# Moving attention coefficients by one pixel: three shift matmuls replaced by two SBUF-to-SBUF transfers per block

## The chip, the core and the metric

The kernel runs on one core of a Trainium2 chip. A core has five engines with instruction queues of their own: TensorE (PE, matmuls, with weight loads shown apart as PEld), VectorE (DVE), ScalarE (ACT), GpSimd (POOL) and SyncE (SP), which here only issues transfers. They run side by side and wait for each other by semaphores. Transfers are carried out by 16 DMA engines. The metric is the device time of one execution in microseconds (us), lower is better.

## What is computed

The reference is a network of two layers on an image batch of 4 x 32 x 32 pixels with 384 channels; each layer is a token mixer ("conv") and a feed-forward part. Only the second layer's mixer, an outlook attention with 12 heads, is touched:

```python
v = jnp.einsum('bhwc,oc->bhwo', x, Wv)
vp = jnp.pad(v, ((0, 0), (1, 1), (1, 1), (0, 0)))
patches = jnp.stack([vp[:, i:i + h, j:j + w] for i in range(3) for j in range(3)], axis=3)
a = jnp.einsum('bhwc,oc->bhwo', x, Wa).reshape(b, n, heads, 9, 9)
attn = jax.nn.softmax(a * d ** (-0.5), axis=-1)
out = jnp.einsum('bnhpq,bnqhd->bnphd', attn, v_unf)
# each of the 9 results p = (i, j) is added to the canvas at offset (i, j), the borders are cut off
y = canvas[:, 1:1 + h, 1:1 + w]
return jnp.einsum('bhwc,oc->bhwo', y, Wo)
```

Each pixel has, per head, 9 x 9 softmax coefficients. What a pixel's output takes from a pixel up to two rows and two columns away is a sum of such coefficients over the centre pixels between them. So the result is a banded product: a band of 25 coefficients per pixel and head times v.

## The kernel before

Before this stage, the first layer's attention (to about 1220 us) and its experts (to about 2358 us) run; after it, the second feed-forward part, which is factored (from about 2825 us). The stage in between is the function `outlook`, from 2360 to 2826 us. It works on blocks of 128 pixels (4 image rows of 32), 8 blocks an image (`NB`), 32 blocks in all; a pixel is a partition. Its parts, each a local function:

- `scores(b, t)`: normalizes the block (`xn`), transposes it on PE (`xnT`), multiplies it with `wa` into PSUM (`ps_a`, L1728), subtracts the maximum (L1737, L1738), takes the exponential on ACT (L1743), sums (L1745 to L1749), takes the inverse (L1750), and multiplies (L1752) into the tile `attn`. It then sends the coefficients of the upper and lower centre rows to the pixels of the image row above or below, that is by 32 partitions: L1764 and L1765 inside the block (96 partitions each), L1767 and L1769 into the neighbouring blocks (32 partitions each). Their targets are the tiles `up` and `down`. It also computes v (L1772, L1776).
- `band(b, t)`: adds what came from above, from below and its own part into `u` (L1785 to L1789), `u` being split by the three horizontal positions of a coefficient. Then three matmuls (L1793) with 128 x 128 shift matrices move the three parts by -1, 0 and +1 pixel, that is by one partition, and add them in PSUM (`ps_c`); the shift matrices have zero rows at the image's edges. DVE copies the result to `co` (L1801) and masks with `inside` what would fall outside of the image. `co` is written to a DRAM area (`room`, L1808), 150 KB, with a row pitch that puts each coefficient where the band wants it; L1814 reads the band back, 1,560 KB, with rows that overlap as memory is read.
- `gather(b, half, t)`: the banded product of v with the band on PE (`ps_y`, L1830). When half an image is complete, ACT copies it to `y` (L1839).
- `mix`: multiplies with `wo` (`ps_wo`, L1846) and adds to x (L1850).
- `add`: for the last blocks, adds the experts' results (gathered by POOL, L1483) to x (L1701).

Steps: a table `later` says which part runs in which step. In step s, `scores` of block s come first, then loads and `add`, then what the table has: `band` of block s - 2, `gather` of block s - 5 (`LAG` = 3), and `mix` after half an image is complete. The order of the instructions on SP and POOL is this program order (`manual_schedule`); on PE, DVE and ACT a planner chooses the order beforehand, and the engine keeps it. [...] SP issues in each step four moves (L1764 to L1769), the room write, which waits for `co`, and the band read, which waits until the room write has landed.

Buffers: `attn` 3, `up` and `down` 4 each, `u` 2, `co` 3, `band` 5, v 7; in PSUM one of `ps_a` (two banks), one of `ps_c`, three of `ps_y`, two shared by `ps_tr`, `ps_v` and `ps_wo`.

Of the kernel before, what the change touches and what calls it, by code (L numbers as in the profile page):

```python
# [1629 lines left out]
def outlook(net, wv, wa, wo, left, router, kron, loads):  # L1630
# [10 lines left out]
    tc, nc = net.tc, net.nc  # L1641
    K2, H6 = 9, NH // 2
    HW_ = K2 * K2 * H6
    PW = K2 * H6
    R = 5 * NH
    with ExitStack() as ctx:
        const = ctx.enter_context(tc.tile_pool(name="ol_const", bufs=1, reuse_waits="tile"))
        work = ctx.enter_context(tc.tile_pool(name="ol_work", bufs=2, reuse_waits="tile"))
        mp = ctx.enter_context(tc.tile_pool(name="ol_moved", bufs=4, reuse_waits="tile"))
        ap_ = ctx.enter_context(tc.tile_pool(name="ol_attn", bufs=3, reuse_waits="tile"))  # L1650
        vp = ctx.enter_context(tc.tile_pool(name="ol_v", bufs=7, reuse_waits="tile"))
        bp = ctx.enter_context(tc.tile_pool(name="ol_band", bufs=5, reuse_waits="tile"))
        ps_m = ctx.enter_context(tc.tile_pool(name="ol_ps_m", bufs=2, space=PSUM, reuse_waits="tile"))
        ps_a = ctx.enter_context(tc.tile_pool(name="ol_ps_a", bufs=1, space=PSUM, reuse_waits="tile"))
        ps_c = ctx.enter_context(tc.tile_pool(name="ol_ps_c", bufs=1, space=PSUM, reuse_waits="tile"))
        ps_y = ctx.enter_context(tc.tile_pool(name="ol_ps_y", bufs=1, space=PSUM, reuse_waits="tile"))


        shift = {}
        for dx in (-1, 0, 1):  # L1660
            m = const.tile([P, P], FP, name=f"shift_{dx}", tag=f"shift_{dx}")
            nc.gpsimd.memset(m, 0.0)
            nc.gpsimd.affine_select(
                out=m, in_=m, compare_op=ALU.not_equal, fill=1.0,
                base=dx, pattern=[[-1, P]], channel_multiplier=1,
            )
            if dx:
                edge = 0 if dx == 1 else IMG - 1
                nc.gpsimd.memset(m.rearrange("p (r x) -> p r x", x=IMG)[:, :, edge : edge + 1], 0.0)
            shift[dx] = m  # L1670

        inside = const.tile([P, 5 * H6], FP, name="inside")
        col = const.tile([P, 4], FP, name="col")
        low = const.tile([P, 5 * H6], FP, name="low")
# [1 line left out]
        def columns():  # L1676
            nc.gpsimd.iota(
                col[:, 0:1], pattern=[[0, 1]], base=0, channel_multiplier=1, allow_small_or_imprecise_dtypes=True,
            )
            for r in range(1, P // IMG):  # L1680
                nc.vector.tensor_scalar(
                    col[:, r : r + 1], col[:, 0:1], IMG * r - 0.5, -float(IMG), ALU.is_gt, ALU.mult
                )
            for r in range(1, P // IMG):
                nc.vector.tensor_tensor(col[:, 0:1], col[:, 0:1], col[:, r : r + 1], ALU.add)
            nc.gpsimd.iota(
                inside, pattern=[[1, 5], [0, H6]], base=-2, channel_multiplier=0,
                allow_small_or_imprecise_dtypes=True,
            )
            nc.vector.tensor_scalar(inside, inside, col[:, 0:1], None, ALU.add)  # L1690
            nc.vector.tensor_scalar(low, inside, -0.5, None, ALU.is_gt)
            nc.vector.tensor_scalar(inside, inside, IMG - 0.5, None, ALU.is_lt)
            nc.vector.tensor_tensor(inside, inside, low, ALU.mult)

        left = list(left)

# [6 lines left out]
                )  # L1703
            net.measure(work, i, net.x(i))

        attn, vs, bands, ys, moved = {}, {}, {}, {}, {}

        def room(b, t):

# [8 lines left out]
        def scores(b, t):  # L1718
# [11 lines left out]
                        start=k == 0, stop=k == KC - 1,  # L1730
                    )

            a = ap_.tile([P, 3, 2, 3, PW], FP, name="attn", tag="attn")
            for hh in range(2):
                mx = work.tile([P, PW], FP, name="a_max", tag="a_max")
                given = pa[:, hh, :HW_].rearrange("p (q e) -> p q e", q=K2)
                nc.vector.tensor_reduce(mx, given.rearrange("p q e -> p e q"), AX.X, ALU.max)  # L1737
                nc.vector.tensor_tensor(  # L1738
                    a[:, :, hh, :, :], given.rearrange("p (y x) e -> p y x e", y=3),
                    mx.unsqueeze(1).unsqueeze(1).to_broadcast([P, 3, 3, PW]), ALU.subtract,  # L1740
                )
            flat = a.rearrange("p y s x e -> p (y s x e)")
            nc.scalar.activation(flat, flat, AF.Exp, scale=QK_SCALE)  # L1743
            rows = work.tile([P, 2, 3, PW], FP, name="a_rows", tag="a_rows", bufs=1)
            nc.vector.tensor_tensor(rows, a[:, 0], a[:, 1], ALU.add)  # L1745
            nc.vector.tensor_tensor(rows, rows, a[:, 2], ALU.add)
            sm = work.tile([P, 2, PW], FP, name="a_sum", tag="a_sum")
            nc.vector.tensor_tensor(sm, rows[:, :, 0, :], rows[:, :, 1, :], ALU.add)
            nc.vector.tensor_tensor(sm, sm, rows[:, :, 2, :], ALU.add)  # L1749
            nc.vector.reciprocal(sm, sm)  # L1750
            for qi in (0, 2, 1):
                nc.vector.tensor_tensor(  # L1752
                    a[:, qi], a[:, qi], sm.unsqueeze(2).to_broadcast([P, 2, 3, PW]), ALU.mult
                )
            attn[b, t] = a


            flat = [a[:, qi].rearrange("p s x e -> p (s x e)") for qi in range(3)]
            if t == 0:
                moved[b, 0] = room(b, 0)  # L1760
            if t + 1 < NB:
# [13 lines left out]
            v = vs[b, t] = vp.tile([P, C], FP, name="v", tag="v")  # L1775
            nc.scalar.copy(v, ps[:, :C])  # L1776

        def band(b, t):


            H3 = 3 * H6
            u = work.tile([P, 6, 5, H3], FP, name="u", tag="u")
            down, up = (m.rearrange("p (g y e) -> p g y e", g=6, y=3) for m in moved.pop((b, t)))
            own = attn.pop((b, t))[:, 1].rearrange("p s x (y e) -> p (s x) y e", y=3)
            nc.scalar.copy(u[:, :, 0, :], down[:, :, 0, :])  # L1785
            nc.scalar.copy(u[:, :, 4, :], up[:, :, 2, :])
            nc.vector.tensor_tensor(u[:, :, 1:3, :], down[:, :, 1:3, :], own[:, :, 0:2, :], ALU.add)
            nc.vector.tensor_tensor(u[:, :, 3, :], own[:, :, 2, :], up[:, :, 1, :], ALU.add)
            nc.vector.tensor_tensor(u[:, :, 2, :], u[:, :, 2, :], up[:, :, 0, :], ALU.add)  # L1789
            pc = ps_c.tile([P, 512], FP, name="ps_c", tag="c")  # L1790
            grid = pc[:, : 5 * R].rearrange("p (s y e) -> p s y e", s=2, y=5)
            for qj in (1, 0, 2):
                nc.tensor.matmul(  # L1793
                    grid[:, :, :, (2 - qj) * H6 : (5 - qj) * H6],
                    lhsT=shift[qj - 1],
                    rhs=u.rearrange("p (s x) y e -> p s x y e", s=2)[:, :, qj, :, :],
                    start=qj == 1, stop=qj == 2, skip_group_check=True,
                )
            co = work.tile([P, 5, 5, NH], FP, name="co", tag="co", bufs=3)
            for hh in range(2):  # L1800
                nc.vector.tensor_tensor(  # L1801
                    co[:, :, :, hh * H6 : (hh + 1) * H6],
                    grid[:, hh].rearrange("p y (x h) -> p y x h", x=5),
                    inside.rearrange("p (x h) -> p x h", x=5).unsqueeze(1).to_broadcast([P, 5, 5, H6]),
                    ALU.mult,
                )
            room = net.room[t]
            nc.sync.dma_start(  # L1808
                out=room.rearrange("(p r) -> p r", p=P)[:, : 5 * IMG * NH]
                .rearrange("p (y r) -> p y r", y=5)[:, :, :R],  # L1810
                in_=co.rearrange("p y x h -> p y (x h)"),
            )
            m = bands[b, t] = bp.tile([P, BAND, NH], FP, name="band", tag="band")
            nc.sync.dma_start(  # L1814
                out=m.rearrange("p t h -> p (t h)"),
                in_=room[: P * BAND * NH].rearrange("(p r) -> p r", p=P),
            )
# [37 lines left out]
        def at(step, f, *args):  # L1855
            later.setdefault(step, []).append((f, args))
# [12 lines left out]
        for b in range(B):  # L1869
            for t in range(NB):  # L1870
                o = b * NB + t
                at(o + 2, band, b, t)
                at(o + 2 + LAG, gathered, b, 0 if t < 5 else 1, t)
                if t == 4:
                    at(o + 2 + LAG, gathered, b, 1, 3)
                    at(o + 2 + LAG, gathered, b, 1, 4)
            for half in range(2):
                done = b * NB + (4 if half == 0 else 7) + 2 + LAG
                for n in range(4):
                    at(done + 1 + n // 2, mixed, b, half, n)  # L1880
        assert left[0] >= 2 * NB
        t_kron, first = 0, left[0]
        for step in range(B * NB + 9):
            b, t = divmod(step, NB)
            if b < B:
                scores(b, t)
            if step == 0:
                columns()
            if step in loads:
                loads[step]()  # L1890
            if step >= 4 and left:
# [340 lines left out]
```

## Time and profile before

| | |
|---|---|
| median of 3 runs | 2922.51 us (2905.18 to 2929.6) |
| profiled execution, its own time | 2919.42 us |
| its span | 2917.6 us |
| PE busy in the span | 2761.2 us (95%) |
| DVE, ACT, POOL busy | 46%, 41%, 14% |
| the stage `outlook` | 2360 to 2826 us, PE busy 441.6 us |
| L1793, the shift matmuls: PE busy in the stage | 35.7 us |
| SP's transfers in the stage, a block | 4 moves, 1 room write, 1 band read |

In a row of a group, the first name is the line, then the engine, the operation, output and inputs, shapes, and the count; behind the bar stand the busy time and the mean of one instruction in ns, behind the next one the idle time of the engine just before them, with what ended it. A row of the timeline has the start, the duration, engine, line, operation, operands and count; what stands in brackets is the idle time before it and what ended it. A row of waits reads: who waited, for whom, us in all, how often, the longest. For SP ("SPq") a duration is that of the issue, not of the transfer.

### The profile page before, as it was taken

How to read it: one execution, taken by the hardware profiler on the slowest of the kernel's cores; microseconds unless marked ns; L12 is line 12 of the kernel's file. 1: busy time of each engine (PE TensorE's matmuls, PEld its weight loads, DVE VectorE, ACT ScalarE, POOL GpSimd, SP SyncE). 2: the span in 40 equal slices, each digit the busy share in tenths (PEclk: the TensorE clock that was granted, in tenths of full speed). 3: DMA queues.
4: the chain of work that ended last, by engine and by line, in shares of the span. 5: the costliest groups of instructions: out<-in, count | busy, mean ns of one | idle time of the engine just before them, and what ended most of it. 6: DMA issues, size and time to landing. Idle time of an engine off the chain costs nothing. (4 is left out here: it accounts for less than half of the span.)

```text
span 2917.6 us, 36735 instructions
## 1 busy us (share of the span) xinstructions
PE 2761.2 (95%) x13236; PEld 1505.9 (52%) x13236; DVE 1347.7 (46%) x3714; ACT 1207.3 (41%) x2023; POOL 400.6 (14%) x499
## 2 busy tenths in 40 slices
PE   6989999999999998699999999999999998999988
PEld 4333333333334332267777777777777754444432
DVE  1376667777777776533000001111111146877642
ACT  3788677677768775211111211211211122122125
POOL 1000000110030004123111122122221101100000
PEclk9999999999999988699999999999999999999999
DMA  5143335223322234345454455555655437544432
GB/s 103 39 115 91 89 90 139 66 62 78 100 55 62 78 79 124 112 163 217 161 195 179 174 203 191 213 201 204 222 190 214 154 130 224 192 154 158 151 105 89
DMA packets 216992, 405.92 MB, mean 139 GB/s; under 512 B 83504, under 2 KB 177904, under 8 KB 203744
## 3 DMA queue, kind: packets, MB, share of 16 engines
q1 hardware_dynamic: 185504, 189.20, 21.6%
q0 software_dynamic: 27152, 209.66, 20.8%
q10 hardware_dynamic: 4144, 4.61, 0.5%
q8 instruction: 107, 1.75, 0.2%
q14 instruction: 85, 0.70, 0.1%
HBM read 305.35 MB, written 49.99 MB: 122 GB/s over the span
## 5 line engine op out<-in xcount | busy, mean ns | idle before, releaser
L1604 ACT ACTIVATE h<-ps_h,up 128x256 f32<-128x256 f32 x420 | 198.6, 473 | 915.2 <-PE ps_h L1600 915.1
L1600 PE MATMUL ps_h<-xbT,up 128*128 128x256 f32 x2520 | 553.2, 380 | 2.6 <-ACT h L1604 1.8
L1617 PE MATMUL ps_y<-down,h 128*128 128x384 f32 x1680 | 554.9, 488 | 0.0
L1600 PEld LDWEIGHTS ps_h<-xbT,up 128*128 128x128 f32 x2520 | 480.7, 191 | 76.7 <-ACT h L1604 2.7
L678 DVE CUSTOM_DVE_ANT_0 e<-e,rz,inv 128x1024 f32<-128x1024 f32 x384 | 475.2, 1274 | 30.0 <-DMA rz<-r_row 30.0
L626 ACT ACTIVATE e<-ps_s,shift 128x1024 f32<-128x1024 f32 x384 | 408.6, 1109 | 81.2 <-PE ps_s L616 48.7
L1617 PEld LDWEIGHTS ps_y<-down,h 128*128 128x128 f32 x1680 | 318.0, 191 | 206.6 <-issue 1.8
L1622 DVE TENSOR_TENSOR y<-ps_y,down 128x384 f32<-128x384 f32 x70 | 39.0, 558 | 721.1 <-PE ps_y L1617 721.1
L616 PE MATMUL ps_s<-q,k 32*128 32x512 f32 x1536 | 279.0, 664 | 36.4 <-ACT e L626 26.7
L634 PE MATMUL ps_o<-e,wv 128*32 128x512 f32 x1536 | 228.4, 670 | 39.3 <-DVE wv L685 36.7
L634 PE MATMUL ps_z<-e,rt_ones 128*32 128x512 f32 x1536 | 218.6, 643 | 0.0
L705 POOL DMA_DIRECT2D q<-po x96 | 76.1, 875 | 958.4 <-DMA q<-po 600.5
L366 ACT ACTIVATE below<-tk_left,tk_bound 128x1024 bf16<-128x1024 f32 (+1 forms) x160 | 184.3, 1152 | 38.0 <-DVE tk_bound L372 31.7
L1728 PE MATMUL ps_a<-wa,xnT 128*128 128x486 f32 x384 | 170.6, 594 | 8.9 <-DVE attn L1738 7.1
L616 PEld LDWEIGHTS ps_s<-q,k 32*128 32x128 f32 x1536 | 84.1, 189 | 168.7 <-ACT e L626 82.6
L281 PE MATMUL ps_t<-xnT,wqkv 128*128 128x512 f32 x288 | 135.4, 611 | 1.1 <-ACT q L520 0.7
L634 PEld LDWEIGHTS ps_o<-e,wv 128*32 128x32 f32 x1536 | 31.7, 112 | 200.3 <-issue 72.6
L1728 PEld LDWEIGHTS ps_a<-wa,xnT 128*128 128x128 f32 x384 | 73.1, 196 | 95.6 <-issue 87.1
L634 PEld LDWEIGHTS ps_z<-e,rt_ones 128*32 128x32 f32 x1536 | 52.7, 118 | 131.1 <-issue 127.1
L1830 PE MATMUL ps_y<-band,v 128*32 128x194 f32 (+2 forms) x960 | 102.7, 516 | 7.2 <-DMA band<-room 6.9
L1569 DVE SCALAR_TENSOR_TENSOR x<-yt,weight,x 128x384 f32<-128x384 f32 x38 | 23.5, 619 | 185.4 <-DMA x<-x 184.7
L1483 POOL DMA_INDIRECT yt<-yg,index x64 | 65.7, 1027 | 304.6 <-DVE x L1569 139.9
(345 smaller groups left out, 2859.2 us busy)
## 6 DMA issues: line engine op xcount, KB each, us to landing
band<-room SPq DMA_DIRECT2D x32, 1560.0 KB
rz<-r_row SPq DMA_DIRECT2D x48, 512.0 KB
yg<-y SPq DMA_DIRECT2D x70, 192.0 KB
q<-q SPq DMA_DIRECT2D x192, 64.0 KB
k<-k SPq DMA_DIRECT2D x192, 64.0 KB
room<-none SPq DMA_DIRECT2D x64, 192.0 KB
x<-x SPq DMA_DIRECT2D x38, 192.0 KB
o<-in_x_dram SPq DMA_DIRECT2D x33, 192.0 KB
```

Source lines behind the costliest of these rows:

```text
L281: nc.tensor.matmul(ps, lhsT=lhsT(k), rhs=rhs(k), start=k == 0, stop=k == KC - 1)
L366: nc.scalar.activation(junk[:n], left[:n], AF.Sign, bias=bound[:n], accum_out=over[:n])
L616: nc.tensor.matmul(ps[:, half * 512 : half * 512 + 512], lhsT=self.k4[r, u * P : (u + 1) * P], rhs=self.q4[r, :], start=True, stop=True,)
L626: nc.scalar.activation(e, ps, AF.Exp, bias=shift, scale=QK_SCALE)
L634: nc.tensor.matmul(ps[r : r + 32, :], lhsT=lhsT(odd), rhs=self.es[2 * u + odd][:, half * 512 : half * 512 + 512], start=u == 0, stop=u == ...
L678: nc.vector.tensor_tensor_reduce(self.es[m], self.es[m], self.rz, 1.0, self.im["inv"][:, m, self.h : self.h + 1], ALU.mult, ALU.add, self. ...
L705: nc.gpsimd.dma_start(out=there, in_=po[r : r + 32, :], accum_op=ALU.add)
L1600: nc.tensor.matmul(ps, lhsT=up[:, o : o + P], rhs=xbT[:, k, :], start=k == 0, stop=k == KC - 1,)
L1604: nc.scalar.activation(h, ps, AF.Gelu, bias=up[:, KC * HID + f : KC * HID + f + 1])
L1617: nc.tensor.matmul(ps, lhsT=hs[f][:, t * P : (t + 1) * P], rhs=down[:, f * C : (f + 1) * C], start=f == 0, stop=f == NF - 1,)
L1728: nc.tensor.matmul(pa[:, hh, :HW_], lhsT=xnT[:, k, :], rhs=wa[:, k, hh * HW_ : (hh + 1) * HW_], start=k == 0, stop=k == KC - 1,)
L1830: nc.tensor.matmul(ys[c][32 * n : 32 * n + 32, lo - 512 * half : hi - 512 * half], lhsT=vs[b, t][:, h * HD : (h + 1) * HD], rhs=bands[b, t ...
```

## The change

The function `band` is cut in two. The new first half, `column(b, t)`, runs in step s for block s - 2; it makes `u` as before and then sends two parts of it to neighbouring pixels: the parts of horizontal position 0 from partitions 1 to 127 to partitions 0 to 126, and those of position 2 from partitions 0 to 126 to partitions 1 to 127. Each is a transfer on SP of 127 partitions with 180 values (720 bytes) in a partition. The targets are two tiles `beside`, used in turn and zeroed once. The new `band` runs one step later, for block s - 3: it builds `co` in SBUF from its own part and the two that have come, with two copies on ACT and four sums on DVE. In a step's order `band` of block s - 3 stands ahead of `column` of block s - 2. `gather` and `mix` run one step later too, so the loop has one step more, and v has 8 buffers in place of 7.

The masks at the image's edges now are multiplied into the inverse of the softmax sums (`edge`, a constant tile made in `columns`), so that coefficients that would leave the image are zero from the start. For that, the inverse is spread over the three horizontal positions (one more product of 324 elements on DVE), and the tile `attn` has its axes in the order position, head group. The three shift matrices, the PSUM tile `ps_c` and the masked copies go. `columns` is called ahead of the first `scores`.

```diff
-        vp = ctx.enter_context(tc.tile_pool(name="ol_v", bufs=7, reuse_waits="tile"))
+        vp = ctx.enter_context(tc.tile_pool(name="ol_v", bufs=8, reuse_waits="tile"))
...
-        shift = {}
-        for dx in (-1, 0, 1):
...
+        H3 = 3 * H6
+        beside = [const.tile([P, 2, 2, 5, H3], FP, name=f"beside_{n}", tag=f"beside_{n}") for n in range(2)]
+        for m in beside:
             nc.gpsimd.memset(m, 0.0)
...
+        edge = const.tile([P, 3, 2 * 3, H3], FP, name="edge")
...
+            targets = inside[:, H6 : 4 * H6].unsqueeze(1).to_broadcast([P, 2 * 3, H3])
+            for qj in range(3):
+                source = inside[:, (qj + 1) * H6 : (qj + 1) * H6 + 1]
+                nc.vector.tensor_scalar(edge[:, qj], targets, source, None, ALU.mult)
...
             nc.vector.reciprocal(sm, sm)
+            nc.vector.tensor_tensor(
+                rows, edge.rearrange("p x (s y) e -> p x s (y e)", s=2),
+                sm.unsqueeze(1).to_broadcast([P, 3, 2, PW]), ALU.mult,
+            )
             for qi in (0, 2, 1):
-                nc.vector.tensor_tensor(
-                    a[:, qi], a[:, qi], sm.unsqueeze(2).to_broadcast([P, 2, 3, PW]), ALU.mult
-                )
+                nc.vector.tensor_tensor(a[:, qi], a[:, qi], rows, ALU.mult)
...
-        def band(b, t):
+        def column(b, t):
...
-            pc = ps_c.tile([P, 512], FP, name="ps_c", tag="c")
-            grid = pc[:, : 5 * R].rearrange("p (s y e) -> p s y e", s=2, y=5)
-            for qj in (1, 0, 2):
-                nc.tensor.matmul(
-                    grid[:, :, :, (2 - qj) * H6 : (5 - qj) * H6],
-                    lhsT=shift[qj - 1],
-                    rhs=u.rearrange("p (s x) y e -> p s x y e", s=2)[:, :, qj, :, :],
-                    start=qj == 1, stop=qj == 2, skip_group_check=True,
-                )
+            m = beside[t % 2].rearrange("p k s y e -> p k (s y e)")
+            nc.sync.dma_start(out=m[: P - 1, 0, :], in_=u[1:, 0:2].rearrange("p s y e -> p (s y e)"))
+            nc.sync.dma_start(out=m[1:, 1, :], in_=u[: P - 1, 4:6].rearrange("p s y e -> p (s y e)"))
+
+        def band(b, t):
+
+            u, m = us.pop((b, t)), beside[t % 2]
             co = work.tile([P, 5, 5, NH], FP, name="co", tag="co", bufs=3)
-            for hh in range(2):
-                nc.vector.tensor_tensor(
-                    co[:, :, :, hh * H6 : (hh + 1) * H6],
-                    grid[:, hh].rearrange("p y (x h) -> p y x h", x=5),
-                    inside.rearrange("p (x h) -> p x h", x=5).unsqueeze(1).to_broadcast([P, 5, 5, H6]),
-                    ALU.mult,
-                )
+
+            def part(source, pj):
+                return source[:, :, :, pj * H6 : (pj + 1) * H6]
+
+            before, own, behind = m[:, 1], u[:, 2:4], m[:, 0]
+            there = [co[:, :, x, :].rearrange("p y (s h) -> p s y h", s=2) for x in range(5)]
+            nc.scalar.copy(there[0], part(before, 0))
+            nc.scalar.copy(there[4], part(behind, 2))
+            for x in (1, 2):
+                nc.vector.tensor_tensor(there[x], part(own, x - 1), part(before, x), ALU.add)
+            nc.vector.tensor_tensor(there[3], part(own, 2), part(behind, 1), ALU.add)
+            nc.vector.tensor_tensor(there[2], there[2], part(behind, 0), ALU.add)
             room = net.room[t]
...
-                at(o + 2, band, b, t)
-                at(o + 2 + LAG, gathered, b, 0 if t < 5 else 1, t)
+                at(o + 3, band, b, t)
+                at(o + 2, column, b, t)
+                at(o + 3 + LAG, gathered, b, 0 if t < 5 else 1, t)
...
-        for step in range(B * NB + 9):
+        columns()
+        for step in range(B * NB + 10):
```

More of the change, by code (lines that the diff above doesn't have):

```diff
@@ L1654, in outlook @@
         ps_a = ctx.enter_context(tc.tile_pool(name="ol_ps_a", bufs=1, space=PSUM, reuse_waits="tile"))
-        ps_c = ctx.enter_context(tc.tile_pool(name="ol_ps_c", bufs=1, space=PSUM, reuse_waits="tile"))
         ps_y = ctx.enter_context(tc.tile_pool(name="ol_ps_y", bufs=1, space=PSUM, reuse_waits="tile"))
-        shift = {}
-        for dx in (-1, 0, 1):
-            m = const.tile([P, P], FP, name=f"shift_{dx}", tag=f"shift_{dx}")
+        H3 = 3 * H6
+        beside = [const.tile([P, 2, 2, 5, H3], FP, name=f"beside_{n}", tag=f"beside_{n}") for n in range(2)]
+        for m in beside:
             nc.gpsimd.memset(m, 0.0)
-            nc.gpsimd.affine_select(
-                out=m, in_=m, compare_op=ALU.not_equal, fill=1.0,
-                base=dx, pattern=[[-1, P]], channel_multiplier=1,
-            )
[L1667 to L1670, printed above, removed]
+        edge = const.tile([P, 3, 2 * 3, H3], FP, name="edge")
         inside = const.tile([P, 5 * H6], FP, name="inside")
@@ L1704, in add @@
             net.measure(work, i, net.x(i))
-        attn, vs, bands, ys, moved = {}, {}, {}, {}, {}
+        attn, us, vs, bands, ys, moved = {}, {}, {}, {}, {}, {}
         def room(b, t):
@@ L1731, in scores @@
                     )
-            a = ap_.tile([P, 3, 2, 3, PW], FP, name="attn", tag="attn")
+            a = ap_.tile([P, 3, 3, 2, PW], FP, name="attn", tag="attn")
             for hh in range(2):
@@ L1738, in scores @@
                 nc.vector.tensor_tensor(
-                    a[:, :, hh, :, :], given.rearrange("p (y x) e -> p y x e", y=3),
+                    a[:, :, :, hh, :], given.rearrange("p (y x) e -> p y x e", y=3),
                     mx.unsqueeze(1).unsqueeze(1).to_broadcast([P, 3, 3, PW]), ALU.subtract,
                 )
-            flat = a.rearrange("p y s x e -> p (y s x e)")
+            flat = a.rearrange("p y x s e -> p (y x s e)")
             nc.scalar.activation(flat, flat, AF.Exp, scale=QK_SCALE)
-            rows = work.tile([P, 2, 3, PW], FP, name="a_rows", tag="a_rows", bufs=1)
+            rows = work.tile([P, 3, 2, PW], FP, name="a_rows", tag="a_rows", bufs=1)
             nc.vector.tensor_tensor(rows, a[:, 0], a[:, 1], ALU.add)
@@ L1747, in scores @@
             sm = work.tile([P, 2, PW], FP, name="a_sum", tag="a_sum")
-            nc.vector.tensor_tensor(sm, rows[:, :, 0, :], rows[:, :, 1, :], ALU.add)
-            nc.vector.tensor_tensor(sm, sm, rows[:, :, 2, :], ALU.add)
+            nc.vector.tensor_tensor(sm, rows[:, 0], rows[:, 1], ALU.add)
+            nc.vector.tensor_tensor(sm, sm, rows[:, 2], ALU.add)
             nc.vector.reciprocal(sm, sm)
+            nc.vector.tensor_tensor(
+                rows, edge.rearrange("p x (s y) e -> p x s (y e)", s=2),
+                sm.unsqueeze(1).to_broadcast([P, 3, 2, PW]), ALU.mult,
+            )
             for qi in (0, 2, 1):
-                nc.vector.tensor_tensor(
-                    a[:, qi], a[:, qi], sm.unsqueeze(2).to_broadcast([P, 2, 3, PW]), ALU.mult
-                )
+                nc.vector.tensor_tensor(a[:, qi], a[:, qi], rows, ALU.mult)
             attn[b, t] = a
-            flat = [a[:, qi].rearrange("p s x e -> p (s x e)") for qi in range(3)]
+            flat = [a[:, qi].rearrange("p x s e -> p (x s e)") for qi in range(3)]
             if t == 0:
@@ L1776, in scores @@
             nc.scalar.copy(v, ps[:, :C])
-        def band(b, t):
-            H3 = 3 * H6
-            u = work.tile([P, 6, 5, H3], FP, name="u", tag="u")
+        def column(b, t):
+            u = us[b, t] = work.tile([P, 6, 5, H3], FP, name="u", tag="u")
             down, up = (m.rearrange("p (g y e) -> p g y e", g=6, y=3) for m in moved.pop((b, t)))
-            own = attn.pop((b, t))[:, 1].rearrange("p s x (y e) -> p (s x) y e", y=3)
+            own = attn.pop((b, t))[:, 1].rearrange("p x s (y e) -> p (x s) y e", y=3)
             nc.scalar.copy(u[:, :, 0, :], down[:, :, 0, :])
@@ L1789, in band @@
             nc.vector.tensor_tensor(u[:, :, 2, :], u[:, :, 2, :], up[:, :, 0, :], ALU.add)
-            pc = ps_c.tile([P, 512], FP, name="ps_c", tag="c")
-            grid = pc[:, : 5 * R].rearrange("p (s y e) -> p s y e", s=2, y=5)
-            for qj in (1, 0, 2):
-                nc.tensor.matmul(
-                    grid[:, :, :, (2 - qj) * H6 : (5 - qj) * H6],
-                    lhsT=shift[qj - 1],
-                    rhs=u.rearrange("p (s x) y e -> p s x y e", s=2)[:, :, qj, :, :],
-                    start=qj == 1, stop=qj == 2, skip_group_check=True,
-                )
-            co = work.tile([P, 5, 5, NH], FP, name="co", tag="co", bufs=3)
-            for hh in range(2):
-                nc.vector.tensor_tensor(
-                    co[:, :, :, hh * H6 : (hh + 1) * H6],
-                    grid[:, hh].rearrange("p y (x h) -> p y x h", x=5),
-                    inside.rearrange("p (x h) -> p x h", x=5).unsqueeze(1).to_broadcast([P, 5, 5, H6]),
-                    ALU.mult,
-                )
+            m = beside[t % 2].rearrange("p k s y e -> p k (s y e)")
[3 more added lines that the diff above has]
+            u, m = us.pop((b, t)), beside[t % 2]
+            co = work.tile([P, 5, 5, NH], FP, name="co", tag="co", bufs=3)
+            def part(source, pj):
[8 more added lines that the diff above has]
+            nc.vector.tensor_tensor(there[2], there[2], part(behind, 0), ALU.add)
             room = net.room[t]
@@ L1871, in outlook @@
                 o = b * NB + t
-                at(o + 2, band, b, t)
-                at(o + 2 + LAG, gathered, b, 0 if t < 5 else 1, t)
+                at(o + 3, band, b, t)
+                at(o + 2, column, b, t)
+                at(o + 3 + LAG, gathered, b, 0 if t < 5 else 1, t)
                 if t == 4:
-                    at(o + 2 + LAG, gathered, b, 1, 3)
-                    at(o + 2 + LAG, gathered, b, 1, 4)
+                    at(o + 3 + LAG, gathered, b, 1, 3)
+                    at(o + 3 + LAG, gathered, b, 1, 4)
             for half in range(2):
-                done = b * NB + (4 if half == 0 else 7) + 2 + LAG
+                done = b * NB + (4 if half == 0 else 7) + 3 + LAG
                 for n in range(4):
@@ L1886, in outlook @@
                 scores(b, t)
-            if step == 0:
-                columns()
             if step in loads:
```

## The prediction

> **What bounds the kernel now.** I read the page first, then the busy time by stretch of the last conv stage (2360 to 2826 us, the only stage that the diff touches), then the chain of waits inside it, the waits of SP's queue, and SP's timeline. The stretches:
>
> ```profile
> 2360.00:2560.00 200.00, 183.51 (x758) 91.53 (x757) 145.82 (x355) 41.46 (x84) 25.37 (x28) 0.96 0.60 187
> 2560.00:2782.00 222.00, 222.00 (x1018) 108.06 (x1019) 156.62 (x395) 51.56 (x100) 1.08 (x3) 1.00 0.47 155
> 2782.00:2826.00 44.00, 36.09 (x248) 18.66 (x241) 21.34 (x56) 6.37 (x11) 0.00 (x0) 0.92 0.41 140
> ```
>
> Columns: stretch, length, then busy us of PE, weight loads, VectorE (DVE), ScalarE (ACT), GpSimd (POOL), granted clock, DMA share, GB/s. PE has no gap at all for 222 us; DVE is busy 71% of it. The stage is PE-bound in its middle, with 16.5 us of PE idle in its head and 8 us in its tail. The groups by form give what the change removes, and the prices I shall use:
>
> ```profile
> L1793 PE MATMUL ps_c<-u,shift 128*128 128x180 f32 x128 | 31.1, 324 | 0.9 <-DVE u L1789 0.9
> L1752 DVE TENSOR_TENSOR attn<-attn,a_sum 128x324 f32<-128x324 f32 x96 | 41.8, 489 | 0.6
> L1801 DVE TENSOR_TENSOR co<-ps_c,inside 128x150 f32<-128x150 f32 x64 | 17.9, 307 | 29.1 <-PE ps_c L1793 29.1
> L1789 DVE TENSOR_TENSOR u<-u,up 128x108 f32<-128x108 f32 x32 | 8.3, 263 | 0.0
> ```
>
> Now the queue that the change adds to. SP issues in program order; one step of its timeline in the steady part, and the drain at the end:
>
> ```profile
> 2647.64 0.54 SPq L1764 DMA_DIRECT2D up<-attn  x1
> 2648.28 0.55 SPq L1765 DMA_DIRECT2D down<-attn  x1
> 2648.88 0.59 SPq L1767 DMA_DIRECT2D up<-attn  x1
> 2649.52 0.58 SPq L1769 DMA_DIRECT2D down<-attn  x1
> 2650.15 0.58 SPq L1808 DMA_DIRECT2D room<-co  x1
> 2652.74 0.33 SPq L1814 DMA_DIRECT2D band<-room  x1
> 2662.90 0.54 SPq L1764 DMA_DIRECT2D up<-attn  x1
> ...
> 2800.34 0.32 SPq L1814 DMA_DIRECT2D band<-room  x1
> 2800.76 0.39 SPq L1808 DMA_DIRECT2D room<-co  x1
> 2807.64 0.32 SPq L1814 DMA_DIRECT2D band<-room  x1
> ```
>
> In the steady step the coefficients' write to DRAM (room) has landed 2.6 us after its issue, and the band's read goes out. In the drain the same room transfer needs 6.9 us, because it stands behind the 1.56 MB band issued 0.4 us earlier. So whatever SP issues right after a band waits for that band. SP itself has room today:
>
> ```profile
> SPq L1764 <- DVE attn L1752: 202.1, 32, 16.1
> SPq L1814 <- DMA room<-co: 91.8, 32, 6.9
> ```
>
> 202.1/32 = 6.3 us a step in which SP only waits for the next coefficients.
>
> [...] Each engine used leaves one 4-byte packet: SP's queue has 1,146 transfers and 17,760 such packets, 576 short of 16 each, which is 48 x 12: the 48 transfers at L650, whose slowest dimension is 4. No transfer of 127 partitions is in it. [...]
>
> **The change, part by part.**
>
> *Removed, PE.* Three shift matmuls a block; from the first to the next instruction's start is 1.02 us in the timeline (2644.73 to 2645.75), 32 x 1.02 = 33 us of the PE-bound stage. That is the gain if nothing else bounds.
>
> *DVE.* The two masked copies go (2 x 0.28 = 0.56 us); the masked inverse comes (324 elements, 0.49), and four sums of 60 elements, [...] 0.88. Net +0.8 us a block, 26 us in all, under DVE's 29% idle while PE bounds; 26 us is its price if that cover is gone, and nothing less than 0 is possible, since no row shortens. The new order of axes leaves every element count as it was. ACT gets two copies of 60 elements, under 0.28 each (108 elements take that), with ACT busy 23%.
>
> *Set-up.* The shift matrices' memsets and selects leave POOL (1.6 us at 2311), two memsets of 360 elements come (an estimate of 0.45 each, from 0.20 for 128 elements), the iotas move ahead of one memset of 0.36; `edge` costs DVE 3 x 0.27. All lie under the experts' last tile, where PE has 48 matmuls from 2342.5 to 2358; without that cover, 2 us. The eighth v buffer pays for the later gather and costs nothing.
>
> *Two transfers a block on SP, and a step more.* Issue: 2 x 0.55 = 1.1 us a step of SP's 6.3 idle. They wait for u of their block, which is long done; behind them on SP stand the next block's four moves, then the room write, which waits for co, which waits for these two transfers. Their data is the dispute. They are [127 partitions x 720 B], [...] 254 packets on the same engine. The packet records give the price of one: 18 ns for 240 B, 56 ns for 1,296 B, 65 for 1,536; the line through the first two gives 35 ns for 720 B, 254 x 35 = 9.0 us. Bounds: the band's 12,480 B take 467 ns, at that rate 720 B would take 27 ns (6.9 us); no more than a 1,296 B packet, 56 ns (14.2 us). I take 9.0.
>
> *The loop that this makes.* SP's order in a step becomes: four moves, room, band, then the two column transfers. A move's landing sets the fixed part: issued at 2648.28, its reader is released at 2650.64, 2.4 us, of which 0.55 is issue and 6 x 56 ns packets; of the other 1.5 I put 1.0 behind the packets. Let a band be issued at 0. Its reader starts 6.6 us later in the drain (2800.34 to 2806.93), so engine 0 is through with it at about 5.6. The column packets end at 14.6 and land at 15.6. co: 4 x 0.22 and a hand-over, 1.0, gives 16.6. Room to band, 2.6: the next band at 19.2. That is the bare cycle; with the packet bounds 17.1 to 24.4. Today a step is 13.3 us ((2787.91 - 2375.97)/31). A longer cycle is possible: co waits on DVE, in order, and the softmax of the next block may stand behind it there (two sums of rows 0.98, two of 0.27, inverse 0.82, masked inverse 0.49, first product 0.49: 3.3 us), and its moves, 2.45 us, stand ahead of the room write on SP. With all of that in the way it is 5.8 us more, with nothing in the way 0; I take half, 3.0: 22.2 us.
>
> *The sum.* The first band goes out at 2402.75 today; its two transfers now come first, behind the x loads, 12 us by the same reckoning: 2415. Then 28 cycles of 22.2 = 622, the last 3, with no softmax left, of 19.2 = 58, and 8 us for the x and weight loads (2.3 MB at the band's rate) that pass between: last band at 3103, against 2807.64 today. From there to the end nothing changes. +295 us on the profiled execution's 2919.4 (span 2917.6; 3 us below the runs' median of 2922.5, which I neglect): **3215 us**. PE's 33 us are not in the sum: PE then waits, with (441.6 - 33)/32 = 12.8 us of work in a step of 22.2.
>
> **The rivals.**
>
> 1. *The transfers spread over 16 engines, or cost little.* Each then has 8 packets an engine, 0.3 us. The cycle would be 5.6 + 0.6 + 1.0 + 1.0 + 2.6 = 10.8, under PE's 12.8, and the PE gain shows: -33, less a longer drain. From the last moves to the last band take 19.7 us today (2787.91 to 2807.64); then it is 4.8 to the first band and three cycles, 37.2: +17.5, of which 5 us are filled by the gather and mix that come a step later; and six steps without gather instead of five, in which DVE has 9.0 us against PE's 7.7, cost 8. -33 + 17.5 - 5 + 8 = -12.5: about 2907. This is the case on the other side (not slower). It decides from the point where both transfers together take under 12.8 - 10.2 = 2.6 us, i.e. from 4 engines on. For it: every other transfer of this stage uses 16. [...]
> 2. *Spread, but DVE's order holds up co.* Rival 1's cycle and the full 5.8 us: 16.6 against 13.3 now, in the blocks where it happens. If a third of them do, 10 x 3.3 = 33 less the 12.5: about 2940.
> 3. *One engine and dearer packets, or further waits of DVE and SP in turn.* 56 ns and 5.8 us: 28 x 30.2 + 3 x 24.4 + 2423 = 3342, 534 later: 3453, and beyond. For it: a quarter of the 1,296 B packets took 81 ns or more. Against: those were among bursts on all engines.
>
> **How the numbers follow.** The forecast with its bounds (packets of 27 to 56 ns, DVE's part 0 to 5.8 us) has 0.82; rival 1 0.07; rival 2 0.05; rival 3 beyond its bound 0.06. The low end is 31 x 17.1 + 2423 = 2953, +145: 3060; the high end, a little inside rival 3's sum, 3430. That holds 8 in 10, all on one side. About 1% is what a measurement of this kernel tells from no change: faster by more than that (below 2893) 0.03, the better part of rival 1; within it 0.09, the rest of rival 1 and rival 2; slower 0.88.
>
> **What would show it.** Right: SP's wait for co turns from 35 us into the largest one, 8 us a step or more; co and the two copies wait for the moved columns by DMA; bands are issued some 22 us apart; PE is busy little over half of the stage; 4-byte packets fall short of 16 a transfer by 64 x 15 more. Each step can fail alone: landing of the columns 9 us behind the band's end (packets), DVE's share (cycle against 19.2). Wrong: the columns land within 8 us of the band's issue, steps stay near 13 us, and PE stays at 100%[...].

## The result and the profile after

The changed kernel takes 3129.21 us (median of 4 runs, 3123.32 to 3139.93) against 2923.01 us (4 runs, 2905.18 to 2929.6) beside it on the same chip: a ratio of 1.073 [1.0701, 1.0759], slower by 206 us. The prediction was 3215 us with a range of 3060 to 3430 and a chance of 0.88 for slower. The profiled execution took 3128.58 us, its span 3126.8 us. The stage begins 4.5 us later than before (first move at 2380.51 us, not 2375.97); the last band goes out at 3019.58 us instead of 2807.64, and 107.2 us later the span ends (110.0 before). So nearly all of the difference lies in the stage that the diff touches, between its first move and its last band.

Two stretches of it, in the columns of the prediction's first view (length, busy us of PE, weight loads, DVE, ACT, POOL, then clock, DMA share, GB/s):

```profile
2460.00:2660.00 200.00, 139.93 (x547) 62.39 (x545) 113.66 (x295) 35.29 (x78) 19.60 (x22) 0.85 0.43 140
2660.00:2860.00 200.00, 146.05 (x608) 67.00 (x609) 109.44 (x293) 37.82 (x85) 0.72 (x2) 0.85 0.37 122
```

PE, 100% busy in the middle of the stage before, is now busy 70 to 73%, and that at a granted clock of 0.85 instead of 1.00. No compute engine is near its limit. DMA, with a share of 0.4, isn't either, but that is an average over 16 DMA engines, and an average can't show one of them being full. What the end waits for is shown by the chain (the page's fourth part, by line):

```profile
DMA beside<-u 6%; SPq L1787 2%; DMA room<-co 2%; SPq L1761 2%; DMA up<-attn 1%; PE ps_h L1998 1%; PE ps_y L2009 1%; SPq L1786 1%; PE ps_o L2025 0%; DMA down<-attn 0%; SPq L1812 0%; DMA out_dram<-o 0%; SPq L1762 0%; DMA band<-room 0%; DMA yt<-yg,index 0%
```

The column transfers (`beside<-u`) lead it with 6% of 3127 us, some 190 us; SP's own time at L1787, the second of their issues, and at L1761, the next block's first move, stands beside them with 2% each. The waits of SP's queue between 2360 and 3040 us (us in total, times, longest):

```profile
SPq L1806 <- DVE co L1804: 122.3, 31, 9.2
SPq L1761 <- DVE attn L1751: 29.7, 4, 15.0
```

Before, SP waited 202 us for the next coefficients (`attn`). Now that is 30 us, and the wait for `co` is the largest: 3.9 us a step. One steady step in SP's timeline (start, length in us, line):

```profile
2701.99 0.33 SPq L1812 DMA_DIRECT2D band<-room  x1
2702.37 0.66 SPq L1786 DMA_DIRECT2D beside<-u  x1
2703.08 5.67 SPq L1787 DMA_DIRECT2D beside<-u  x1
2708.80 4.31 SPq L1761 DMA_DIRECT2D up<-attn  x1
2713.15 0.59 SPq L1762 DMA_DIRECT2D down<-attn  x1
2713.79 0.59 SPq L1764 DMA_DIRECT2D up<-attn  x1
2714.43 0.94 SPq L1766 DMA_DIRECT2D down<-attn  x1
2718.02 0.38 SPq L1806 DMA_DIRECT2D room<-co  x1
2720.80 0.33 SPq L1812 DMA_DIRECT2D band<-room  x1
```

From band to band 18.8 us (13.3 before). Two of SP's issues are long: a move's issue took about 0.55 us in the kernel before; here the issue of the second column transfer takes 5.67 us and that of the first move behind it 4.31 us, and the trace has no wait for a semaphore in them. What the columns released is in the timeline of DVE and ACT:

```profile
2708.44 1.31 DVE L1751 TENSOR_TENSOR attn<-attn,a_rows 128x324 f32<-128x324 f32 x3
2713.18 0.24 ACT L1800 COPY co<-beside 128x60 f32<-128x60 f32 x1 [7.83 <-DMA beside<-u]
2717.00 0.24 ACT L1799 COPY co<-beside 128x60 f32<-128x60 f32 x1 [3.57 <-DMA beside<-u]
2717.74 0.20 DVE L1804 TENSOR_TENSOR co<-co,beside 128x60 f32<-128x60 f32 x1
```

The first columns are usable 11.2 us after the band's issue (2701.99 to 2713.18), the second 15.0 us after it (2717.00), and 1 us later `co` is complete and `room` goes out. DVE had done the next block's softmax products (L1751) before the first columns came, so nothing of DVE's order was in the way here. Nor was it in the other blocks: in nearly all of them DVE stood idle until the columns came.

```profile
DVE co L1802 <- DMA beside<-u: 118.7, 31, 7.6
```

**How many engines carry the columns.** The packet records show it in two ways. By the 4-byte packets: in the kernel before, the four moves of a block (256 packets of 1,296 B) leave 64 of them, 16 a transfer, and a transfer of 4 partitions (L650) leaves 4 behind its 4 packets of 2,048 B. SP's queue now has 1,210 transfers and 17,824 such packets: short of 16 each by 1,536, which is the 576 of before plus 64 x 15 = 960, so a column transfer leaves one. And by the order in time: of the band's packets 16 run at once for half of the time, of the columns' never more than two, the second beginning a few ns before the first ends. So each of the 64 column transfers used one engine. Which of the 16 it was, the records don't say; the prediction and the expectations call it engine 0. The 8,128 column packets of 720 B take 35 ns each (median); the 254 of a block follow one another and are through in 8.3 us, 32.7 ns apart. In the step above the last 16 of the moves' 256 packets, as many as fall to one engine, go out one after another from 2716.65 to 2717.52 us; the last column packet ends at 2716.64.

### The profile page after: what moved, and what is told of

It reads as the page before. It is cut to its first block, busy times and chain, and to the rows that moved or that the text cites. A ratio compares the mean times of both kernels' runs of the same rounds, so it can differ in the third digit from the quotient of the medians.

```text
span 3126.8 us, 36639 instructions
## 1 busy us (share of the span) xinstructions
PE 2767.3 (89%) x13044; PEld 1489.6 (48%) x13044; DVE 1369.5 (44%) x3813; ACT 1222.6 (39%) x2087; POOL 401.4 (13%) x493
## 5 line engine op out<-in xcount | busy, mean ns | idle before, releaser
L1723 PE MATMUL ps_a<-wa,xnT 128*128 128x486 f32 x384 | 191.0, 654 | 56.2 <-DVE attn L1733 43.9
L1828 PE MATMUL ps_y<-band,v 128*32 128x194 f32 (+2 forms) x960 | 91.2, 518 | 91.9 <-DMA band<-room 65.3
L1723 PEld LDWEIGHTS ps_a<-wa,xnT 128*128 128x128 f32 x384 | 83.2, 223 | 152.4 <-issue 127.6
L1769 PE MATMUL ps_v<-wv,xnT 128*128 128x384 f32 x192 | 82.2, 564 | 44.8 <-ACT xnT L151 42.7
```

What stands on the lines that cost most here:

```text
L1723: nc.tensor.matmul(pa[:, hh, :HW_], lhsT=xnT[:, k, :], rhs=wa[:, k, hh * HW_ : (hh + 1) * HW_], start=k == 0, stop=k == KC - 1,)
L1769: nc.tensor.matmul(ps[:, :C], lhsT=xnT[:, k, :], rhs=wv[:, k, :], start=k == 0, stop=k == KC - 1)
L1828: nc.tensor.matmul(ys[c][32 * n : 32 * n + 32, lo - 512 * half : hi - 512 * half], lhsT=vs[b, t][:, h * HD : (h + 1) * HD], rhs=bands[b, t ...
```

## The experiments

All edits are to the changed kernel, and each run is compared with the kernel before on the same chip (2921 to 2923 us in every case). The planner chose the order on PE, DVE and ACT anew for each version, so a difference of a few us between two of them can be that. The stage's first move, ahead of all columns, goes out between 2373 and 2387 us in these runs.

**1 and 2: the same columns on more engines.** Each transfer is cut into 112 + 15 partitions, or into 124 + 3; place and order stay.

```
-nc.sync.dma_start(out=m[: P - 1, 0, :], in_=u[1:, 0:2]...)
-nc.sync.dma_start(out=m[1:, 1, :], in_=u[: P - 1, 4:6]...)
+for lo, hi in ((0, 112), (112, 127)):      # second kernel: ((0, 124), (124, 127))
+    nc.sync.dma_start(out=m[lo:hi, 0, :], in_=u[lo + 1 : hi + 1, 0:2]...)
+    nc.sync.dma_start(out=m[lo + 1 : hi + 1, 1, :], in_=u[lo:hi, 4:6]...)
```

> The changed kernel with each 127-partition transfer cut in two, 112 and 15 partitions, four transfers a block in place of two, the same bytes. Theory (one DMA engine carries all 254 packets): 112 partitions spread over 16 engines and 15 over 15, at most 16 packets an engine for both directions, 0.6 us in place of 8.3; the loop on SP falls from 18.6 us to about 11, under the 12.8 us of PE work a block, so PE bounds again: 2907 us (2890 to 2930), SP's issues of the columns 0.55 us each instead of 5 to 6. Rival (the order on SP is the cost: the columns stand between a band and a room write, and co waits for both, however fast they are): two more issues make it worse or leave it, above 3080 us.

> The same with 124 and 3 partitions: 124 spreads over 4 engines, 3 over 3, so 64 packets on the busiest engine, 2.1 us at 33 ns. Theory: loop of 5.6 + 2.1 + 1.0 + 1.0 + 2.6 = 12.3 us plus what the issues block, about PE's 12.8: 2915 us (2895 to 2950). Rival (order on SP): above 3080 us, and no difference from the cut at 112.

112 + 15 took 2962.82 us, ratio 1.0148 [1.0115, 1.018]; 124 + 3 took 2970.26 us, ratio 1.0177 [1.0144, 1.0209]. The 4-byte packets (19,744 and 18,208) come to 31 and 7 for each column transfer that was cut, where it had left one: 16 + 15 and 4 + 3 engines. The 254 data packets of a block now take 1.7 and 2.6 us instead of 8.3. So 166 of the 206 us were the single engine, and the 7 us between 4 and 16 engines are too few to be told from the planner's order. But both numbers miss: 2907 and 2915 were expected, with ranges up to 2930 and 2950. SP's waits and the timelines of the first kernel tell why:

```profile
SPq L1807 <- DVE co L1805: 107.6, 32, 10.9
```

```profile
2628.95 0.33 SPq L1813 DMA_DIRECT2D band<-room  x1
...
2641.43 0.39 SPq L1807 DMA_DIRECT2D room<-co  x1
2645.03 0.33 SPq L1813 DMA_DIRECT2D band<-room  x1
```

```profile
2636.91 0.24 ACT L1801 COPY co<-beside 128x60 f32<-128x60 f32 x1 [6.84 <-DMA beside<-u]
...
2640.75 0.48 DVE L142 TENSOR_SCALAR xn<-x,mv_x,rs_x 128x384 f32<-128x384 f32 x1 [1.31 <-PE ps_tr L150]
```

The wait for `co` is still there. The band's 5.6 us (the prediction's estimate) stand ahead of the columns on every engine; ACT gets its columns at 2636.91, 8.0 us after the band, and the last sum of `co` (L1805) starts on DVE only at 2641.15. That is the kind of delay that the prediction's second rival has (spread, but DVE's order holds `co`: about 2940), though not with the instructions that it named: the next block's softmax products (L1751) were over when the columns came. What stood between was the addition of `mix` and the statistics behind it (L1849, L123, L1961), then `xn` of a later block (L142), which itself waited 1.3 us for PE. The first rival (2907) isn't reached by spreading alone.

**3: no column transfers.** Both lines are left out, so `beside` stays zero and the coefficients of the left and right neighbours are missing from the result; everything else is done.

> The changed kernel without the column transfers: the tiles beside stay zero, so the parts from the neighbouring columns are left out of the result; all else is as in the changed kernel. It gives what the removal of the matmuls and the later band are worth when the move is free. Theory: PE bounds, -33 us for the matmuls, +7 for the drain with one band more, -5 for PE work in it, +8 in the head: 2900 us (2885 to 2920). Rival (DVE's four sums, the masked inverse and the ACT copies are the cost, not the transfers): above 3050 us.

2888.71 us, ratio 0.9884 [0.9848, 0.9921]: 32 us under the kernel before, within the range expected. This is a net figure: the matmuls are gone, DVE and ACT have their added instructions, and the loop has its step more. It is as large as the 33 us that the prediction gave for PE alone, so the additions cost little or nothing as long as no transfer is waited for. The transfers cost 3129 - 2889 = 240 us.

**4: the columns issued by POOL**, 127 partitions each (`nc.gpsimd.dma_start` in both lines).

> The two 127-partition transfers as they are, but issued by POOL instead of SP. Theory: [...] then the data takes 0.3 us a transfer and the time falls to PE's bound, if POOL's order (gathers of the experts' results that wait for DVE stand ahead of the columns) does not hold them up: 2915 us (2895 to 2980). If it is one engine there too, or the rival (order on SP) is not the cause, the columns still take 8 us: 3000 us and above.

2951.76 us, ratio 1.0113 [1.0082, 1.0144], in the upper half of the range expected. That POOL's transfers would spread over 16 engines was the author's assumption, and the packets bear it out: POOL's queue has 2,048 data packets more, and per transfer they are 16 of 4,320 B, 15 of 1,440 B and one of 724 B, which is 8 rows of 720 B for each of 15 engines and 7 rows, with 4 bytes more, for the last. SP waits for coefficients again (257.5 us in 30 waits for `attn`), but ACT waits 117.1 us for columns. In one step they are issued at 2644.02, 1.6 us after a band, and usable 5.9 us later. How much of that is the band ahead of them and how much POOL's way of issuing, this run doesn't tell.

**5 and 6: the columns ahead of the band.** The columns of block s - 2 are issued before the band of block s - 3, by registering them in the table of steps first; in the fifth kernel with 112 + 15 partitions, in the sixth with 127.

```
+for o in range(B * NB):
+    at(o + 2, column, *divmod(o, NB))
 ...
-        at(o + 2, column, b, t)
```

> The cut at 112 and 15 partitions, and in each step the column transfers of block s - 2 ahead of the band of block s - 3 on SP, nothing else. The cut alone left 2963 us, with bands 13.1 us apart on SP and co waiting for columns that stand behind a band. Theory (what is left after the cut is that wait: the columns stand behind 5.6 us of band): ahead of the band they land about 2.5 us after their issue, co is done long before the next room write, SP is back to 9 us of work a step and PE bounds: 2895 us (2880 to 2915), close to the 2889 us without any transfer. Rival (four more transfers, or DVE's and ACT's additional work, cost by themselves): 2940 us or more.

> The changed kernel with only that order: the two 127-partition transfers ahead of the band, still on one engine. Theory: the wait of co goes, but engine 0 still carries per block 8.3 us of columns, 4.0 of its share of the band, 0.9 of moves and 0.7 of room, 14 us against PE's 12.8, and the room write lands behind the columns: 2960 us (2930 to 3010). Rival (the order is all, one engine or 16 does not matter then): 2895 us. Rival (the engine is all): 3100 us.

The fifth took 2907.97 us, ratio 0.9949 [0.9931, 0.9968], within the range expected, and beats the kernel before by half a per cent: little, but the whole interval lies below 1. SP's wait for `co` has all but gone, and PE is at 96%:

```profile
SPq L1807 <- DVE co L1805: 18.1, 6, 11.5
```

```profile
2560.00:2760.00 200.00, 191.16 (x917) 88.81 (x915) 165.79 (x448) 52.35 (x129) 1.51 (x4) 1.00 0.59 185
```

The sixth, with the order alone changed, took 3077.17 us, ratio 1.0523 [1.0497, 1.0549], where 2960 (up to 3010) was expected; the rival by which the single engine is all (3100) comes nearer. SP's timeline:

```profile
2708.66 0.66 SPq L1786 DMA_DIRECT2D beside<-u  x1
2709.36 3.60 SPq L1787 DMA_DIRECT2D beside<-u  x1
2713.05 4.36 SPq L1806 DMA_DIRECT2D room<-co  x1
2722.17 0.33 SPq L1812 DMA_DIRECT2D band<-room  x1
```

I had reckoned that columns which `co` doesn't need yet can be late at no cost. But the room write of the other block, which now comes right behind them, has its own part on that engine: its issue is held for 4.36 us, and it has landed only 9.1 us after the issue began.

**7: columns made, but not read.** The transfers stay as they are; the additions and copies read a third tile of zeros (`still`), so the result again lacks the neighbours' coefficients.

> The changed kernel in which band reads a third tile of zeros in place of what has come, so that the parts of the neighbouring columns are left out of the result, while the two transfers of 127 partitions are still made. It takes away co's wait and leaves the load on SP and on engine 0. Theory: SP's own issues are held while engine 0 works the columns off (5.5 and 4 us in the changed kernel), so the moves are through 13 us after the band, and room and band follow: a cycle of about 15.5 us against 19: 3015 us (2970 to 3060). Rival (only the wait of co for the columns costs): 2895 us.

3066.77 us, ratio 1.0501 [1.0478, 1.0524]. The rival's 2895 is out: the transfers cost 178 us (3066.77 - 2888.71) though no instruction reads what they bring. It is also just over the range of my own theory. SP's timeline:

```profile
2689.99 0.33 SPq L1814 DMA_DIRECT2D band<-room  x1
2690.42 0.66 SPq L1788 DMA_DIRECT2D beside<-u  x1
2691.14 5.51 SPq L1789 DMA_DIRECT2D beside<-u  x1
2696.83 3.91 SPq L1763 DMA_DIRECT2D up<-attn  x1
...
2703.00 0.58 SPq L1808 DMA_DIRECT2D room<-co  x1
2706.95 0.33 SPq L1814 DMA_DIRECT2D band<-room  x1
```

```profile
ACT u L1782 <- DMA beside<-u: 212.3, 26, 15.4
```

SP is held twice in its issues and comes out of them 10.8 us after the band (2700.74); then come the moves, the room write, which needs no wait for `co`, and its landing: 17.0 us from band to band. The sequence of packets on the one engine comes near this: 5.6 us of band, 8.3 of columns, 0.9 of moves, some 0.7 of room (these last two worked out from the packet prices in the prediction), and about 1.0 of landing, together 16.5. One wait for the columns is left in this kernel: ACT and DVE can't write a later block's `u` into a buffer that the transfers still read, and ACT stood idle 212.3 us for that. In the step shown SP waits for neither of them, only for the landing of its own room write, so this wait doesn't make the cycle there.

**8 and 9: the columns issued by ACT's queue**, in the changed kernel's order, with 112 + 15 partitions or with 127.

```
-nc.sync.dma_start(...)
+nc.scalar.dma_start(...)
```

> The cut at 112 and 15 partitions, issued by ACT's queue in place of SP's, in the changed kernel's order. Theory (what is left after the cut is that the columns stand in SP's ring behind a band and that SP's next moves stand behind them): on ACT's ring they go out as soon as u is there, and SP keeps its old work: 2900 us (2885 to 2915), as with the columns ahead of the band on SP (2908) or better. ACT pays about 2.8 us of issue a block, with 25% of it busy. Rival (ACT's issues delay the exponential and the copies that PE waits for): 2930 us or more.

> The two transfers of 127 partitions as they are, issued by ACT's queue. One engine still carries them, but in another ring than the moves, room and band. Theory (the one engine's work is what bounds, in which ring ever): band 4.0, columns 8.3, moves 0.9, room 0.7, about 14 us a block on that engine against PE's 12.8, and the two rings share it: 2985 us (2950 to 3040). Rival (the order in SP's ring alone makes the cycle): 2905 us. Rival (the wait of co for the columns makes it): 3060 us and above.

2938.17 us, ratio 1.0057 [1.0042, 1.0072], and 3202.81 us, ratio 1.0962 [1.0922, 1.1001]. Both miss. The eighth lies where its rival had it (2930 or more), the ninth far above its theory (2985), in the open range of the rival by which `co`'s wait makes the cycle (3060 and above). SP is free again in the eighth (192.2 us of waits for `attn`), but ACT's copies for `co` wait 79.7 us for columns, and `xnT` and v, which don't need the columns, are released by them too (19.9 and 13.3 us). ACT's work is held up, as the expectation's rival had it. In the ninth ACT is held by its issues, as SP was:

```profile
2825.27 5.52 ACTq L1787 DMA_DIRECT2D beside<-u  x1
2830.83 1.01 ACT L1738 ACTIVATE attn<-attn 128x972 f32<-128x972 f32 x1 [7.80 <-issue]
```

```profile
ACT co L1800 <- DMA beside<-u: 199.7, 25, 20.7
```

The exponential (L1738) starts when the issue ends. The copies then wait for the columns at the head of ACT's queue, and what stands behind them is late for PE: its matmuls of v wait 89.9 us for `xnT`, the weight loads of `ps_a` 86.2 us. The ninth kernel was to tell the order on SP's queue from the load of the one engine; ACT's trouble covers that, and it doesn't.

## Why the prediction was right, and where it was off

**One engine: right.** It was the author's assumption: the trace before has no transfer of 127 partitions. The packets after show it, and experiment 1 gives its price, 166 us. Crossing it with the order:

| | columns behind the band | columns ahead of it |
|---|---|---|
| one engine | 3129 | 3077 |
| 16 and 15 engines | 2963 | 2908 |

The engines are worth 166 or 169 us, the order 52 or 55: the two add up to within a few us, and neither alone brings the kernel back to 2922. That they agree to 3 us is closer than these runs can hold. Counted from the stage's first move to its last band in the four profiled executions (639, 585, 466 and 418 us), the engines are worth 173 or 167 us and the order 54 or 48.

**Price of a packet: right.** 35 ns predicted and recorded; 9.0 us a block predicted, 8.3 measured.

**PE's gain, and DVE's instructions hidden: right as a sum.** Experiment 3: -32 us. The four sums, for which the prediction has the author's estimate of 0.22 us each, took 0.22 (medians of the three lines 0.215 to 0.222).

**The loop: right in its links, with one that I had not seen.** Columns on hand were forecast 15.6 us after the band and came at 15.0; room 16.6, measured 16.0; next band 19.2, measured 18.8 in the step shown. I closed the loop through the wait for `co` alone, and for that wait I named 8 us a step or more as a sign. It came to 3.9, because SP spent some 9 us of each steady step held in two issues. Experiment 7 shows that without that wait the cycle is only some 2 us shorter, because SP is held in its issues and its later transfers stand behind the columns on the same engine. The runs split the difference so: -32 (matmuls gone, experiment 3), +178 (transfers made, experiment 7 less 3), +62 (`co` waits for them, the changed kernel less experiment 7). These are differences from one run to the next, so that they add up (+208, against 206) is no proof of the parts.

**DVE's share of the cycle: the term that was mis-sized.** "I take half, 3.0" of 5.8 us, times 28 steps: 84 us. Measured: about nothing. From the eighth gap on, bands are 18.1 to 20.5 us apart with a median of 18.7, under the bare 19.2; only the first seven are longer, by 14 us together. DVE waited for the columns in 31 blocks, and in the step shown the products of the next block's softmax (L1751) were done some 3 us before the first columns landed (2708.44 + 1.31 against 2713.18). With 0 in its place the sum gives 3215 - 84 = 3131 us against 3128.6. That closeness is partly luck, since small errors cancel in it: the first band came at 2420 instead of 2415, the cycles from there took 599 us instead of 604, and the end came 2.8 us sooner behind the last band. The half was a middle between two bounds. The loop's own times spoke for the low one: with `co` waiting for columns until 15 us after the band, DVE, busy 55% of a step here, has time for the next block's softmax before they land.

**Rival 1's number** (2907) is reached only with both edits, the cut and the order: 2908 in experiment 5. Its sum was for the old order, so that the two agree to 1 us is chance. With the cut alone it is the kind of case that **rival 2** describes, at 2963 some 23 us above its 2940: `co` is held in DVE's order after the columns have come. In the changed kernel this didn't show, because its columns come later than the instructions that could have held `co`.

Open: why experiment 5 is still 19 us above experiment 3, whose transfers are left out (four issues more a step on SP, and a wait for `co` of 18 us in all, are candidates; no run tells them apart); and, with ACT's queue, what a second queue on the same engine would give if its issuer had nothing else to do.

## What to carry to other kernels

Before work of PE is given to a transfer, find out how many engines that transfer uses: here 127 partitions, issued by SP, ran on one and took 8.3 us a block, 124 + 3 on 4 and 3 and took 2.6, 112 + 15 on 16 and 15 and took 1.7. Then look at what stands ahead of it in the queue: behind a band, those 1.7 us of columns were usable only 8.0 us after the band in the step shown of experiment 1, and only the cut together with the place ahead of the band beat the matmuls (2908 us against 2922). A transfer whose data nobody reads was not free either: it cost 178 us here (experiment 7 less 3), delayed what was issued behind it, and held SP in its issue (5.51 us in the step shown).

## What was not expected of the hardware

- Issues on SP were long where 127 packets of the transfer before still had to go through one engine: 4.8 to 7.0 us for the second column transfer, and 3.9 to 4.8 us for the first move behind it in 28 of the 32 steps, against about 0.55 us for a move before. With 112 + 15 partitions the columns' issues take 0.5 to 1.0 us, one of them 2.6 us. The trace shows the length of the issue, not its cause. On ACT's queue the same happened, up to 8.3 us (experiment 9), and in the step shown there ACT's exponential came after the issue (2830.83 us, the issue's end being at 2830.79).
- 720-byte packets from SBUF to SBUF follow each other on one engine every 32.7 ns, with 35 ns recorded for each.
- In these stretches of the stage PE's granted clock was lower where PE had more gaps: 0.99 to 1.00 with PE busy 96 to 100% (the kernel before, experiments 3 and 5), 0.85 with 70 to 73% (the changed kernel), 0.77 with 60% (experiment 6, 2860 to 2960 us).
